# Block-diagonal products of a four-layer GNN, made in parts of the TensorE array instead of over zero blocks

## The chip, the cores and the metric

One NeuronCore of a Trainium2 chip. The metric is device time in us of one execution; lower is better. Times are medians of several executions; all executions quoted here were in the fast state. "PE" is the matmul engine (TensorE), "PEld" its loads of stationary matrices, DVE VectorE, ACT ScalarE, POOL GpSimd.

## The reference

128 graphs of 64 nodes with 256 features pass through four layers, each `x = x + layer(relu(layernorm(x)), adj)`. What the change touches in them is the product with something that is 64 x 64 for each graph:

```python
# layer 0 (4 heads of 64 features), layer 1 (1 head of 256): attention inside a graph
Hout = einsum('bijh,bjhf->bihf', softmax(...), Wh)
# layer 2: one relation ("loop") that selects edges with adj == 1
out = out + einsum('bnm,bmd->bnd', (adj_t == 1), vals)     # per graph
# layer 3: three rounds of a GRU over the graph
A = (adj != 0)
for i in range(3):
    m = h @ weight[i]
    aggr = einsum('bst,bsd->btd', A, m)                    # A^T per graph
    h = gru_cell(aggr, h, w_ih, w_hh, b_ih, b_hh)
```

(The kernel forms A^T h first and multiplies by `weight[i] @ w_ih.T` afterwards.)

## The kernel before

Everything is fp32. Two graphs share the 128 partitions ("a pair"), four pairs make a group, 16 groups go through the kernel. A planner written in the kernel records all operations, gives each an estimated cost and a due time, and emits them in a static order for every engine, so that attention layers of later groups fill the gaps of the GRU rounds ("the loop") of the group in front. Each fp32 matmul appears in the trace as two passes.

The products above were made for a pair at once, with a 128 x 128 matrix that has the two graphs on its diagonal and zeros elsewhere; such matrices are cleared once and only their diagonal blocks are written:

```python
def along(psum, hnat, abd, aT, c):             # A^T h, half c of the features
    pa = psum.tile([P, T], F32, name="tp")     # P = 128, T = 512
    for p in range(G):                         # G = 4 pairs
        nc.tensor.matmul(pa[:, p*P:(p+1)*P], hnat[:, p, c*P:(c+1)*P], abd[:, p, :], start=True, stop=True)
    nc.scalar.copy(aT[:, c, :], pa)

def aggregate(work, psum, lhsT, wv, heads):    # attention
    for p in range(n):
        po = psum.tile([P, 512], F32, name="mm")
        for h in range(heads):
            nc.tensor.matmul(pv[:, h, :], lhsT(p, h), wv[:, p, h, :], start=True, stop=True)
        # ... divide by the row of sums ...

# loop relation (layer 2)
    for i in range(2):
        nc.tensor.matmul(po[:, i, :], oh[:, p, :], v[:, p, :], start=True, stop=True)
```

In `along` the stationary operand is 128 nodes x 128 features of `hnat` and the moving one 128 nodes x 128 columns of `abd`. In attention the stationary operand is the 128 x 128 block matrix and 65 columns (four heads) or 257 (one head) move. The kernel uses eight banks of PSUM, the memory to which PE writes its results: five belong to named gates of the GRU, three are shared by all the rest.

## Time and profile before

| | kernel before |
|---|---|
| time, median | 1485.5 us (1484.1 to 1486.6) |
| span of the profiled run | 1483.7 us |
| busy: PE, DVE, ACT, POOL | 97%, 73%, 52%, 41% |
| steady period of a group (stores 1 to 12) | (1167.3 - 215.1) / 11 = 86.56 us |
| first store of a result | at 215.1 us |
| waits of PE between 215 and 1337 us | 0.6 us in all |

The row to read first is the last: in the middle PE runs without a stop, so any time that its stream gives or takes shows in the period. The prediction below shows the lines. One thing more is seen in the timeline of PE and PEld (columns: start, length, engine, what, count of passes):

```profile
722.67 0.60 PE L372 MATMUL rz<-aS,wc 128*128 128x256 f32 x2
722.89 1.08 PEld L372 LDWEIGHTS tp<-abd,hnat 128*128 128x128 f32 x8
```

The eight loads for an A^T h product begin at 722.89, while the pass before still runs; the first of its matmuls starts at 723.11. In a stream that uses the whole array, loads lie beneath running passes.

### The profile page before, as it was taken

To read this page: it belongs to the slowest core of one execution; us is meant where nothing else is said; L and a number is where in the kernel's file an instruction comes from. 1 tells how busy PE (TensorE), PEld (TensorE's weight loads), DVE (VectorE), ACT (ScalarE), POOL (GpSimd) and SP (SyncE) were. 2 spreads that over 40 slices of the span, in tenths; PEclk is the share of its full clock that TensorE was granted. 3 is DMA by queue.
4 is the path that set the end of the run, shared out by engine and by line. 5 is a ranking of instruction groups with operands and counts; after the bars stand their busy time and mean duration, and the time that the engine had idled before them with its cause. 6 is when DMAs were issued, how large, how long until landed. Compare 5 with 4: busy or idle time off the path is not lost.

```text
span 1483.7 us, 21159 instructions
## 1 busy us (share of the span) xinstructions
PE 1442.3 (97%) x6389; PEld 1065.7 (72%) x6389; DVE 1080.6 (73%) x2823; ACT 766.4 (52%) x1789; POOL 604.0 (41%) x752
## 2 busy tenths in 40 slices
PE   5979999999999999999999999999999999999997
PEld 4656777767777677777767777776777777676764
DVE  7667677786868778686877868687786868675644
ACT  3644645545454555545455554545555454554543
POOL 3522624433443454343345435334543433452522
PEclk7989999999999999999999999999999999999998
DMA  7010121122223122222312222231212222111000
GB/s 202 19 22 19 34 60 25 40 53 48 57 40 72 27 46 49 40 63 40 72 27 46 49 41 62 40 72 24 46 32 40 48 36 58 18 19 29 15 15 17
DMA packets 289635, 65.37 MB, mean 44 GB/s; under 512 B 265448, under 2 KB 287720, under 8 KB 289512
## 3 DMA queue, kind: packets, MB, share of 16 engines
q1 hardware_dynamic: 288952, 63.40, 20.2%
q8 instruction: 54, 0.88, 0.3%
q10 hardware_dynamic: 560, 0.52, 0.1%
q14 instruction: 69, 0.57, 0.1%
HBM read 25.96 MB, written 8.53 MB: 23 GB/s over the span
## 4 chain that ended last, share of the span: by engine, by line
PE 90%; DVE 6%; ACT 2%; SPq 1%; issue 1%; POOL 0%; DMA 0%; DVEq 0%; ACTq 0%
PE mm L372 22%; PE ry L372 22%; PE nh L372 11%; PE ni L372 10%; PE rz L372 10%; PE tp L372 9%; PE rm L372 5%; DVE hn L372 1%; DVE st L372 1%; SPq L372 1%; ACT hn L372 1%; DVE hT L372 1%; DVE d L372 0%; DVE o L372 0%; DVE z L372 0%
## 5 line engine op out<-in xcount | busy, mean ns | idle before, releaser
L372 POOL TENSOR_TENSOR d<-hT,t 128x256 f32<-128x256 f32 x192 | 151.7, 797 | 410.7 <-ACT t L372 410.7
L372 PE MATMUL ni<-aT,wc 128*128 128x512 f32 x384 | 195.7, 593 | 0.1
L372 PE MATMUL nh<-hT,whh 128*128 128x512 f32 x384 | 193.6, 593 | 0.0
L372 ACT COPY z<-ry 128x256 f32<-128x256 f32 x192 | 70.9, 369 | 188.0 <-PE ry L372 146.6
L372 DVE SCALAR_TENSOR_TENSOR t<-r,t 128x256 f32<-128x256 f32 x192 | 89.6, 467 | 90.4 <-ACT r L372 66.6
L372 ACT ACTIVATE z<-z,brz 128x256 f32<-128x256 f32 x192 | 96.8, 504 | 88.4 <-DVE z L372 86.4
L372 DVE TENSOR_TENSOR z<-rz,z 128x256 f32<-128x256 f32 x192 | 80.9, 421 | 78.6 <-PE rz L372 60.5
L372 POOL TENSOR_TENSOR xg<-xg,hn 128x1024 f32<-128x1024 f32 (+1 forms) x32 | 73.0, 2280 | 146.7 <-DVE hn L372 146.7
L372 DVE SCALAR_TENSOR_TENSOR d<-z,d 128x256 f32<-128x256 f32 x192 | 93.3, 506 | 33.2 <-ACT z L372 22.6
L372 PE MATMUL mm<-wl,hT 128*128 128x512 f32 x248 | 117.0, 593 | 0.2 <-ACT t L372 0.2
L372 PE MATMUL rz<-hS,whh 128*128 128x256 f32 x384 | 114.9, 381 | 1.9 <-DVE z L372 1.9
L372 ACT ACTIVATE hn<-xg,var,rstd 128x256 f32<-128x256 f32 x200 | 107.9, 594 | 16.8 <-DVE var L372 15.8
L372 PE MATMUL ry<-hS,wsum 128*128 128x256 f32 x384 | 115.6, 383 | 0.5 <-ACT z L372 0.5
L372 PE MATMUL ry<-aS,wsum 128*128 128x256 f32 x384 | 114.4, 380 | 0.0
L372 PE MATMUL rz<-aS,wc 128*128 128x256 f32 x384 | 114.3, 379 | 0.0
L372 PEld LDWEIGHTS tp<-abd,hnat 128*128 128x128 f32 x768 | 102.2, 192 | 15.4 <-issue 4.3
L372 POOL TENSOR_TENSOR hS<-hT 128x256 f32<-128x256 f32 x96 | 70.6, 741 | 96.2 <-PE ry L372 76.2
L372 PEld LDWEIGHTS ry<-hS,wsum 128*128 128x128 f32 x384 | 70.0, 190 | 54.8 <-issue 30.6
L372 ACT ACTIVATE t<-t,bi 128x256 f32<-128x256 f32 x192 | 93.6, 502 | 27.6 <-DVE t L372 26.7
L372 PE MATMUL tp<-abd,hnat 128*128 128x128 f32 x768 | 106.0, 275 | 0.0
L372 PEld LDWEIGHTS mm<-wh,eb 128*128 128x128 f32 x620 | 86.3, 195 | 18.9 <-issue 7.8
L372 DVE SCALAR_TENSOR_TENSOR hT<-d,t 128x256 f32<-128x256 f32 x192 | 95.8, 520 | 3.3
(192 smaller groups left out, 3193.6 us busy)
## 6 DMA issues: line engine op xcount, KB each, us to landing
hT<-hn SPq DMA_DIRECT2D x896, 32.0 KB
out_dram<-hnat SPq DMA_DIRECT2D x16, 512.0 KB
xg<-in_x_dram SPq DMA_DIRECT2D x15, 512.0 KB
hT<-row SPq DMA_DIRECT2D x28, 256.0 KB
at<-in_adj_dram SPq DMA_DIRECT2D x64, 32.0 KB
ag<-in_adj_dram SPq DMA_DIRECT2D x16, 128.0 KB
t<-row SPq DMA_DIRECT2D x28, 64.0 KB
ihn<-in_L_gnn_w_ih_dram SPq DMA_DIRECT2D x1, 768.0 KB
```

Of the source, the lines that this page charges most:

```text
L372: return do(*[real(a) for a in args], **{k: real(v) for k, v in kwargs.items()})
```

## The change

Its intent: compute only the diagonal blocks. TensorE can be used in parts. In the traces below a matmul whose operands lie on partitions 0 to 63 or 64 to 127 is listed with 64 rows of the array (`64*128`), one that also writes only 64 output partitions with 64 columns too (`64*64`), and several such products run side by side, with starts 0.007 us apart. So `A^T h` is made in two row parts (64 nodes each, 128 stationary columns), attention and the loop relation in four parts of 64 x 64. The change gives row parts that run at once different PSUM banks, so each set of products that are issued together (a "bundle") takes two of the three shared banks. The zero blocks, and the memsets that cleared them, go; the order of graphs within a group is changed so that the four parts meet. Core of the diff:

```diff
+    def beside(products, cost):        # emit all products of a bundle together, as one operation of the planner
     def along(psum, hnat, abd, aT, c):
-        pa = psum.tile([P, T], F32, name="tp")
+        pa, pb = psum.tile([P, G, N], F32, name="tp"), psum.tile([P, G, N], F32, name="tq")
+        products = []
         for p in range(G):
-            nc.tensor.matmul(
-                pa[:, p * P : (p + 1) * P], hnat[:, p, c * P : (c + 1) * P], abd[:, p, :],
-                start=True, stop=True,
-            )
-        nc.scalar.copy(aT[:, c, :], pa)
+            for half, ps in ((0, pa), (1, pb)):
+                b = slice(half * N, (half + 1) * N)
+                products.append((ps[:, p, :], hnat[b, p, c * P : (c + 1) * P], abd[b, p, :]))
+        beside(products, 700.0)
+        to = aT[:, c, :].rearrange("p (g a j) -> p a g j", a=2, j=N)
+        nc.scalar.copy(to[:, 0], pa)
+        nc.scalar.copy(to[:, 1], pb)
+    def aggregate_graphs(work, psum, t, wv, heads):
+        for u in range(n // 2):
+            banks = [psum.tile([P, 512], F32, name=name) for name in ("mm", "mn")]
+            for h in range(heads):
+                for a in range(2):
+                    for r in range(2):
+                        b, s, to = slice(r * N, (r + 1) * N), 2 * u + a, slice(a * N, (a + 1) * N)
+                        products.append((pv[r][to, h, :], t[b, s * heads + h, :], wv[b, s, h, :]))
+            beside(products, 800.0 if heads > 1 else 600.0)
# loop relation: likewise, one bundle of eight products in four parts
+            beside(products, 1050.0 * n / 4)
# planner: costs above; due times tuned anew
-        start, period = 88.0, 87.9
+        start, period = 94.8, 82.2
-    LATENCY = 165.1
+    LATENCY = 176.7
# (cut: layouts of hT and the edges, one more load of edges, min over 128 partitions at once)
```

More of the change, by code (lines that the diff above doesn't have):

```diff
@@ L152, in tile, with place @@
         return View(base, shape, (), [(0, n) for n in shape], list(range(len(shape))))
-    def place(self, base):
+    def place(self, base, taken):
         if self.real is None:
@@ L160, in place, with released @@
         live = [b for b in self.live.get(base.tag, ()) if b.left]
-        return base.tag if len(live) < base.bufs else None
-    def released(self, tag, base):
+        return base.tag if len(live) + taken.count(base.tag) < base.bufs else None
+    def released(self, tag, base, before):
         live = self.live.get(tag, ())
-        if len(live) < self.room(tag, base):
+        before -= self.room(tag, base) - len(live)
+        if before < 0:
             return 0.0
-        return min(b.end for b in live if not b.left) + Plan.LATENCY
+        return sorted(b.end for b in live if not b.left)[before] + Plan.LATENCY
     def room(self, tag, base):
@@ L220, in __getattr__, with all_of @@
         return getattr(self.nc, name)
+    @staticmethod
+    def all_of(view):
+        shape = view.base.make[0]
+        return View(view.base, shape, (), [(0, n) for n in shape], list(range(len(shape))))
     def kept(self, pool, shape, dtype, name):
@@ L317, in emit @@
                         if b.real is None:
-                            tag = b.pool.place(b)
+                            taken = [tag for x, tag in places.items() if x.pool is b.pool]
+                            tag = b.pool.place(b, taken)
                             if tag is None:
@@ L321, in emit @@
                             places[b] = tag
-                            t = max(t, b.pool.released(tag, b))
+                            t = max(t, b.pool.released(tag, b, taken.count(tag)))
                     else:
@@ L464 @@
     ar = adj.rearrange("b n m -> (b n) m").rearrange("(t q) m -> q t m", q=P)
-    tr = adj.rearrange("(u a g) i j -> a i u g j", a=2, g=2)
+    tr = adj.rearrange("(t r a) i j -> t a i r j", r=2, a=2)
+    er = adj.rearrange("(t r a) j i -> t r j a i", r=2, a=2)
     outr = out.rearrange("b n d -> (b n) d").rearrange("(t q) d -> q t d", q=P)
@@ L486, with by_graph, pair, layernorm_T @@
     brz = nc.kept(const, [P, 4], F32, name="brz")
-    def layernorm_T(work, psum, src, hT, natural=None):
+    def by_graph(hT):
+        return hT.rearrange("p k t -> p (k t)").rearrange("p (a k m j) -> p a k m j", a=2, k=K, j=N)
+    def pair(hT, k, s):
+        return by_graph(hT)[:, s % 2, k, s // 2 * 2 : s // 2 * 2 + 2].rearrange("p r j -> p (r j)")
+    def layernorm_T(work, psum, src, hT, natural=None, graphs=False):
         n = src.shape[1]
@@ L510, in layernorm_T, with layernorm_T_by_dma @@
                 nc.tensor.transpose(pt[:, p * P : (p + 1) * P], hn[:, p, k * P : (k + 1) * P], ident)
-            nc.scalar.activation(hT[:, k, :], pt[:, : n * P], AF.Relu)
+            to, out = hT[:, k, :], pt[:, : n * P]
+            if graphs:
+                to = by_graph(hT)[:, :, k]
+                out = out.rearrange("p (m a j) -> p a m j", a=2, j=N)
+            nc.scalar.activation(to, out, AF.Relu)
         if natural is not None:
             nc.vector.tensor_scalar(natural, hn, 0.0, None, op0=ALU.max)
-    def layernorm_T_by_dma(work, src, hT, natural=None):
+    def layernorm_T_by_dma(work, src, hT, natural=None, graphs=False):
         n = src.shape[1]
@@ L535, in layernorm_T_by_dma @@
             for j in range(P // S):
-                turned = hT[j * S : (j + 1) * S].rearrange("p k (n i c) -> p (k n) i c", n=n, c=S)
-                blocks = tb[i * S : (i + 1) * S].rearrange("p k n q -> p (k n) q")
-                nc.sync.dma_start(turned[:, :, i, :], blocks[:, :, j * S : (j + 1) * S])
+                turned, blocks = hT[j * S : (j + 1) * S], tb[i * S : (i + 1) * S]
+                if graphs:
+                    turned = by_graph(turned).rearrange("p a k m (b c) -> p a b (k m) c", b=2)[:, i // 2, i % 2]
+                else:
+                    turned = turned.rearrange("p k (n i c) -> p (k n) i c", n=n, c=S)[:, :, i]
+                blocks = blocks.rearrange("p k n q -> p (k n) q")
+                nc.sync.dma_start(turned, blocks[:, :, j * S : (j + 1) * S])
     def transpose_blocks(psum, dst, src, rblocks, scale=1.0):
@@ L567, in relational_weights, with emit @@
             nc.scalar.copy(w[:, f, D:], pm[:, :D])
+    def beside(products, cost):
+        def emit():
+            for product in products:
+                nc.nc.tensor.matmul(*[real(x) for x in product], start=True, stop=True)
+        if not nc.on:
+            return emit()
+        writes = list({id(x[0].base): x[0] for x in products}.values())
+        nc.note("PE", emit, cost, [Plan.all_of(x) for x in writes], [x for p in products for x in p[1:]])
     def elu_add(work, src, o, engine):
@@ L581, in block_diagonal, with values @@
             nc.vector.tensor_scalar(dst[b, :, b], src[b], scalar, None, op0=op)
-    def values(work, psum, src, heads, we, by_dma=False):
+    def values(work, psum, src, heads, we, by_dma=False, graphs=False):
         fo = D // heads
@@ L588, in values @@
         if by_dma:
-            layernorm_T_by_dma(work, src, hT)
+            layernorm_T_by_dma(work, src, hT, graphs=graphs)
         else:
-            layernorm_T(work, psum, src, hT)
+            layernorm_T(work, psum, src, hT, graphs=graphs)
         wh = work.tile([P, n, D + heads], F32, name="wh")
@@ L599, in values @@
                 nc.tensor.matmul(
-                    pm[:, : D + 2 * heads], hT[:, k, p * P : (p + 1) * P], we[:, k, :],
+                    pm[:, : D + 2 * heads], pair(hT, k, p) if graphs else hT[:, k, p * P : (p + 1) * P], we[:, k, :],
                     start=(k == 0), stop=(k == K - 1),
@@ L622, in aggregate @@
         return o.rearrange("p g h f -> p g (h f)")
+    def aggregate_graphs(work, psum, t, wv, heads):
+        fo = D // heads
+        n = wv.shape[1]
+        o = work.tile([P, n, heads, fo], F32, name="o")
+        for u in range(n // 2):
+            banks = [psum.tile([P, 512], F32, name=name) for name in ("mm", "mn")]
+            pv = [po[:, : D + heads].rearrange("p (h f) -> p h f", h=heads) for po in banks]
+            products = []
[5 more added lines that the diff above has]
+            beside(products, 800.0 if heads > 1 else 600.0)
+            for r in range(2):
+                rec = work.tile([P, heads], F32, name="rec")
+                nc.vector.reciprocal(rec, pv[r][:, :, fo])
+                nc.vector.tensor_tensor(
+                    o[:, 2 * u + r], pv[r][:, :, :fo], rec[:, :, None].to_broadcast([P, heads, fo]), ALU.mult
+                )
+        return o.rearrange("p g h f -> p g (h f)")
     def along(psum, hnat, abd, aT, c):
-        pa = psum.tile([P, T], F32, name="tp")
+        pa, pb = psum.tile([P, G, N], F32, name="tp"), psum.tile([P, G, N], F32, name="tq")
+        products = []
         for p in range(G):
-            nc.tensor.matmul(
-                pa[:, p * P : (p + 1) * P], hnat[:, p, c * P : (c + 1) * P], abd[:, p, :],
-                start=True, stop=True,
-            )
-        nc.scalar.copy(aT[:, c, :], pa)
+            for half, ps in ((0, pa), (1, pb)):
[5 more added lines that the diff above has]
+        nc.scalar.copy(to[:, 1], pb)
         return 0.9
@@ L667, in before_recurrence @@
             layernorm_T(work, psum, src, hT, natural=hnat)
-        block_diagonal(abd, adjacency, 0.0, ALU.not_equal)
+        nc.vector.tensor_scalar(abd, adjacency, 0.0, None, op0=ALU.not_equal)
         aT = work.tile([P, K, T], F32, name="aT")
@@ L877, in tile, with place @@
                 return view
-            def place(self, base):
+            def place(self, base, taken):
                 if base.tag in self.own:
-                    return super().place(base)
+                    return super().place(base, taken)
                 for tag in ("mt", *self.own) if self.early else ("mt",):
-                    if sum(1 for b in self.live.get(tag, ()) if b.left) < self.room(tag, base):
+                    live = sum(1 for b in self.live.get(tag, ()) if b.left)
+                    if live + taken.count(tag) < self.room(tag, base):
                         return tag
@@ L920 @@
         nc.scalar.dma_start(w0e[:, :, :D], rows(W0))
-        AT, XG, AG = [], [], []
+        AT, XG, AG, EG = [], [], [], []
         def load_group(g):
@@ L931, in load_group @@
                 for u in range(G // 2):
-                    nc.sync.dma_start(at[a * N : (a + 1) * N, u], tr[a][:, g * G // 2 + u])
+                    edges = tr[g * G // 2 + u, a]
+                    nc.sync.dma_start(at[a * N : (a + 1) * N, u], edges)
             AT.append(at)
@@ L939, in load_edges @@
             AG.append(ag)
+            eg = work.tile([P, G, N], I32, name="eg", bufs=2)
+            for r in range(2):
+                for u in range(G // 2):
+                    nc.sync.dma_start(eg[r * N : (r + 1) * N, 2 * u : 2 * u + 2], er[g * G // 2 + u, r])
+            EG.append(eg)
         bl = once.tile([P, 2 * D], F32, name="bl")
@@ L979, in attention_columns @@
                 )
-        unset = []
-        def blocks(name, n, pool=once):
-            t = pool.tile([P, n, P], F32, name=name)
-            unset.append(t)
-            return t
-        EB = [blocks("eb0", G * H), blocks("eb1", G)]
         wl = once.tile([P, K, 2 * D], F32, name="wl")
@@ L1009, in edge_bounds, with attention @@
             return mt
-        def attention(g, p0, n, layer, heads, we, pool, eb):
+        def attention(g, p0, n, layer, heads, we, pool):
             nh = n * heads
             src = XG[g][:, p0 : p0 + n]
-            wv, es = values(pool, psum, src, heads, we, g >= AHEAD)
+            wv, es = values(pool, psum, src, heads, we, g >= AHEAD, True)
             if layer == 0 and p0 == 0:
@@ L1023, in attention @@
             nc.scalar.activation(gd, es[:, :, heads:], AF.Exp, scale=ALPHA)
-            t = pool.tile([P, nh, N], F32, name="hT" if heads > 1 else "t")
+            t = pool.tile([P, nh, N], F32, name="t")
             if g < AHEAD:
@@ L1064, in attention @@
                 nc.vector.tensor_tensor(t[:, c], t[:, c], flat(fd, c), ALU.max)
-                for half in range(2):
-                    b = slice(half * N, (half + 1) * N)
-                    nc.vector.tensor_tensor(
-                        eb[b, c, b].rearrange("p (g h) i -> p g h i", g=m),
-                        t[b, c].rearrange("p (g h) i -> p g h i", g=m),
-                        mt[b, q : q + m, None, :].to_broadcast([N, m, heads, N]),
-                        ALU.min,
-                    )
-            o = aggregate(pool, psum, lambda p, h: eb[:, p * heads + h, :], wv, heads)
+                t4 = t[:, c].rearrange("p (g h) i -> p g h i", g=m)
+                edges = mt[:, q : q + m, None, :].to_broadcast([P, m, heads, N])
+                nc.vector.tensor_tensor(t4, t4, edges, ALU.min)
+            o = aggregate_graphs(pool, psum, t, wv, heads)
             elu_add(pool, src, o, nc.vector if g < 1 else nc.gpsimd)
-        def clear():
-            for t in unset:
-                nc.gpsimd.memset(t, 0.0)
         def first_weights():
@@ L1114, in loop_relation @@
             if g >= AHEAD:
-                layernorm_T_by_dma(pool, src, hT)
+                layernorm_T_by_dma(pool, src, hT, graphs=True)
             else:
-                layernorm_T(pool, psum, src, hT)
-            oh = OH[g % 2][:, p0 : p0 + n]
-            block_diagonal(oh, AG[g][:, p0 : p0 + n], 1.0, ALU.is_equal)
+                layernorm_T(pool, psum, src, hT, graphs=True)
+            oh = pool.tile([P, n, N], F32, name="oh")
+            nc.vector.tensor_scalar(oh, EG[g][:, p0 : p0 + n], 1.0, None, op0=ALU.is_equal)
             v = pool.tile([P, n, D], F32, name="v")
@@ L1123, in loop_relation @@
                 for k in range(K):
-                    nc.tensor.matmul(pm, hT[:, k, p * P : (p + 1) * P], wl[:, k, :], start=(k == 0), stop=(k == K - 1))
+                    nc.tensor.matmul(pm, pair(hT, k, p), wl[:, k, :], start=(k == 0), stop=(k == K - 1))
                 u = pool.tile([P, 2 * D], F32, name="u")
@@ L1128, in loop_relation @@
                 nc.vector.scalar_tensor_tensor(v[:, p, :], u[:, D:], 1.0, u[:, :D], op0=ALU.add, op1=ALU.mult)
-            for q in range(n // 2):
-                po = psum.tile([P, 2, D], F32, name="mm")
-                ps = slice(2 * q, 2 * q + 2)
-                for i in range(2):
-                    p = 2 * q + i
-                    nc.tensor.matmul(po[:, i, :], oh[:, p, :], v[:, p, :], start=True, stop=True)
-                nc.vector.scalar_tensor_tensor(src[:, ps, :], po, 0.0, src[:, ps, :], op0=ALU.max, op1=ALU.add)
-        MT, START = {}, {}
+            po = [psum.tile([P, n // 2, D], F32, name=name) for name in ("mm", "mn")]
+            products = []
+            for u in range(n // 2):
+                for a in range(2):
+                    for r in range(2):
+                        b, s = slice(r * N, (r + 1) * N), 2 * u + a
+                        products.append((po[r][a * N : (a + 1) * N, u, :], oh[b, s, :], v[b, s, :]))
+            beside(products, 1050.0 * n / 4)
+            for r in range(2):
+                to = src.rearrange("p (u r) d -> p r u d", r=2)[:, r]
+                nc.vector.scalar_tensor_tensor(to, po[r], 0.0, to, op0=ALU.max, op1=ALU.add)
+        MT, START, ABD = {}, {}, {}
         EARLY = [Layer(f"{i}e", early, {}) for i in range(3)]
-        EBE = [blocks("eb0e", 2 * H, early), blocks("eb1e", 2, early)]
-        OH = [blocks(f"oh{i}", G) for i in range(2)]
-        ABD = [blocks(f"abd{i}", G) for i in range(2)]
         def first_layer(g, p0, n, spare):
@@ L1146, in first_layer @@
                 pass
-            attention(g, p0, n, 0, H, w0e, *((EARLY[0], EBE[0]) if spare else (W[0], EB[0])))
+            attention(g, p0, n, 0, H, w0e, EARLY[0] if spare else W[0])
         def second_layer(g, p0, n, spare):
-            attention(g, p0, n, 1, 1, w1e, *((EARLY[1], EBE[1]) if spare else (W[1], EB[1])))
+            attention(g, p0, n, 1, 1, w1e, EARLY[1] if spare else W[1])
         def third_layer(g, p0, n, spare):
@@ L1164, in before @@
         def before(g):
-            START[g] = before_recurrence(W[3], psum, XG[g], AG[g], ABD[g % 2], g >= AHEAD)
+            ABD[g] = work.tile([P, G, N], F32, name="abd")
+            START[g] = before_recurrence(W[3], psum, XG[g], AG[g], ABD[g], g >= AHEAD)
         def recur(g):
             recurrence(
-                W[3], psum, START.pop(g), XG[g], ABD[g % 2],
+                W[3], psum, START.pop(g), XG[g], ABD[g],
                 lambda h: nc.sync.dma_start(outr[:, g * G : (g + 1) * G, :], h),
             )
-        nc.begin("clear")
-        clear()
         nc.begin("columns")
         first_weights()
-        nc.begin("weights", 18.0, 82.0)
+        nc.begin("weights", 18.0, 84.9)
         later_weights(early)
         layers = (first_layer, second_layer, third_layer)
-        start, period = 88.0, 87.9
+        start, period = 94.8, 82.2
         users = {}
@@ L1186 @@
             if g == 0:
-                units = [(0, 2, (3.7, 29.0, 52.5, 72.6)), (2, 2, (3.7, 31.0, 57.4, 75.8))]
+                units = [(0, 2, (-3.0, 30.1, 57.3, 72.2)), (2, 2, (4.1, 32.9, 59.6, 78.0))]
             elif g == 1:
-                units = [(0, 2, (26.1, 54.4, 86.1, 103.1)), (2, 2, (47.2, 70.3, 95.7, 123.8))]
+                units = [(0, 2, (28.7, 55.8, 87.9, 107.3)), (2, 2, (46.0, 70.1, 100.9, 126.4))]
             elif g == 2:
-                units = [(0, G, (76.1, 115.1, 174.5, 238.3))]
+                units = [(0, G, (74.9, 112.9, 175.1, 237.8))]
             else:
-                end = start + g * period - 25.0
-                units = [(0, G, [end - 63.0 * i for i in (3, 2, 1, 0)])]
+                end = start + g * period - 28.8
+                units = [(0, G, [end - 52.1 * i for i in (3, 2, 1, 0)])]
             for p0, n, at in units:
@@ L1205 @@
             at = start + g * period
-            nc.begin(("before", g), at - (13.0 if g == 0 else 18.9), at, [("recur", g - 2)] if g > 1 else [])
+            nc.begin(("before", g), at - (13.0 if g == 0 else 17.8), at, [("recur", g - 2)] if g > 1 else [])
             before(g)
@@ L1246, in general @@
                 psum = s3.enter_context(tc.tile_pool(name="gru_ps", bufs=1, space=PSUM))
-                abd = one.tile([P, G, P], F32, name="abd")
-                nc.gpsimd.memset(abd, 0.0)
+                abd = one.tile([P, G, N], F32, name="abd")
                 with tc.For_i(0, NP, G) as p0:
```

## The prediction

> **What bounds the kernel now.** I read the page first, then the table of stretches, the waits of the matmul engine, and its timeline in the middle of the run. The page names the engine:
>
> ```profile
> PE 1442.3 (97%) x6389; PEld 1065.7 (72%) x6389; DVE 1080.6 (73%) x2823; ACT 766.4 (52%) x1789; POOL 604.0 (41%) x752
> ```
>
> Busy time of pipelined matmuls is modelled, so I checked by stretches whether PE ever idles. I cut them where one group's result is stored and the next group's loop starts (the stores lie 86.5 us apart in the middle). Columns: length, then busy us of PE, PEld, DVE, ACT, POOL.
>
> ```profile
> 0.00:125.00 125.00, 100.33 (x410) 69.03 (x411) 86.08 (x258) 60.54 (x157) 47.30 (x73) 0.89 0.29 77
> ...
> 648.20:734.70 86.50, 86.50 (x390) 64.75 (x389) 65.66 (x174) 45.74 (x107) 36.58 (x44) 1.00 0.24 48
> 734.70:821.20 86.50, 86.50 (x390) 64.74 (x389) 65.64 (x174) 45.75 (x107) 36.58 (x44) 1.00 0.23 48
> ...
> 1412.00:1484.00 72.00, 59.66 (x253) 42.22 (x251) 30.61 (x68) 29.42 (x64) 20.48 (x28) 0.95 0.05 17
> ```
>
> In the middle PE never stops for a whole group and runs at full clock; the next engine, DVE, is busy 66 of 86.5 us. Between 215 and 1337 us the waits of PE come to two of 0.3 us. Only the first 125 us (25 us idle) and the last 72 us (12 us idle) are partly bound by latency. So in the middle, time taken from PE's stream comes off the span one for one, until DVE at about 66 us per group.
>
> What the changed products cost is read from starts in PE's timeline, not from busy times (columns: start, length, work; x counts passes, as each fp32 matmul appears as two instructions):
>
> ```profile
> 707.76 1.47 PE L372 MATMUL mm<-wh,eb 128*128 128x257 f32 x6
> 709.07 1.02 PE L372 MATMUL nh<-hT,whh 128*128 128x512 f32 x2
> 709.92 0.60 PE L372 MATMUL mm<-wh,eb 128*128 128x257 f32 x2
> 710.36 0.60 PE L372 MATMUL ry<-hT,wsum 128*128 128x256 f32 x2
> 710.79 0.59 PE L372 MATMUL rm<-aT,wc 128*128 128x256 f32 x2
> ...
> 723.11 1.05 PE L372 MATMUL tp<-abd,hnat 128*128 128x128 f32 x8
> 724.00 0.38 PE L372 MATMUL tp<-ident,m 128*128 128x128 f32 x2
> ...
> 736.38 2.91 PE L372 MATMUL mm<-wh,eb 128*128 128x65 f32 x24
> 739.12 0.65 PE L372 MATMUL ry<-hT,wsum 128*128 128x256 f32 x2
> 739.61 0.59 PE L372 MATMUL rm<-hT,whh 128*128 128x256 f32 x2
> 740.04 1.00 PE L372 MATMUL mm<-wh,eb 128*128 128x65 f32 x8
> 740.88 0.65 PE L372 MATMUL ry<-aT,wsum 128*128 128x256 f32 x2
> ```
>
> A pass over 512 columns costs 0.43 us (709.07 to 709.92 for two), over 256 columns 0.216, over 128 columns 0.111 (0.89 for eight): 0.84 ns a column. But 65 columns cost 0.114 (2.74 for 24), as much as 128. There the loading of a stationary matrix of 128 columns sets the pace, not the moving one.
>
> **What the Trainium skill says.** (1) "TensorE: Matmul & The Clock Gate", section "LDWEIGHTS (loading the stationary operand)": the load takes time by its columns, about 107 ns for 128, whatever the number of rows. The 0.114 us of the 65-column passes agrees. (2) The same page, "What overlaps and what doesn't" under "The mechanism": small products on different parts of the array run at once, with starts some 4 ns apart, but matmuls start and end in program order. No run yet shows this here. (3) The same page, section "Wait — 56ns, not 53.3ns?": starts are never closer than about 25 ns. The trace agrees: four tiny passes (`wq`, 10 columns, one stationary column) begin 26 ns apart. (4) "TensorEngine Tiling (Array Packing)", "Key Properties" and "Restrictions and Gotchas": changing the tiling drains the array, and row parts must write different PSUM banks. The kernel before has no tiling, so its trace cannot say what a drain costs; a lone pass of 128 columns lasts 0.275 us against a spacing of 0.111, so I estimate 0.16 us.
>
> **The change part by part.** Per group of four pairs of graphs, with a cost now and after. For "after" I use the costs that the diff itself gives its scheduler for the new bundles (0.70, 0.80, 0.60, 1.05 us). The scheduler's costs for old matmuls (118 ns a pass at least, 427 ns for 256 columns) are within some 5% of the trace, so I take these as fitted too, and check each against array time plus one drain.
>
> A^T h: six bundles a group (three layers, two halves). Now 8 passes, 0.89 us each, 5.34 in all. After: 16 passes over 64 columns, two row halves at once: 8 x 64 x 0.84 ns = 0.43, plus 0.16 is 0.59; the diff says 0.70. I take 0.70: 4.20 in all.
>
> Attention of four heads: now 32 passes, 2.74 + 0.84 = 3.58 us. After: two bundles of 32 passes, each at the 26 ns floor: 0.83; the diff says 0.80. 1.60 in all.
>
> Attention of one head: now 8 passes, 1.31 + 0.44 = 1.75. After: two bundles of 8 passes, four at once: 2 x 0.217 + 0.16 = 0.60, as the diff says. 1.20 in all.
>
> Loop relation: now 8 passes of 256 columns, 8 x 0.216 = 1.73. After: one bundle of 16 passes, four at once: 4 x 0.216 + 0.16 = 1.03; the diff says 1.05.
>
> Sum: 5.34 + 3.58 + 1.75 + 1.73 = 12.40 us now, 8.05 after: 4.35 us less a group, so a steady period of 82.15 instead of 86.5. Over 16 groups: 69.6 us.
>
> What lies beside it: ACT copies A^T h in two pieces of 256 columns instead of one of 512 (0.37 against 0.585 us a copy: 0.155 us more, six times a group; ACT is at 46 of 86.5). DVE does the `min` of attention and the edge masks once over 128 partitions instead of twice over 64: 4 x 0.686 + 2 x 0.42 + 4 x 0.285 us a group are halved, some 2.4 us less. Four small loads of edges a group are added, against DMA busy 24%. The clearing of zero blocks goes from POOL, about 5.8 us at the start; the first scale factor does not wait for it (POOL is idle 1.54 us before it), so nothing is gained there. None of this is on PE's path.
>
> What is taken off: group 0, and part of group 1, do their attention and loop products in the first 125 us, where PE idles anyway; of their 2 x 3.2 us I count half as lost, 3 us. Bundles need two of the three shared PSUM banks at once, where one was enough; for that I allow 0.2 us a group, 3 us. So 69.6 - 6 is about 64 us, and 1485.5 - 64 = 1421. The due times in the diff go from a period of 87.9 to 82.2, a little more than my 4.35; that pulls me down slightly, to **1418 us**.
>
> **The rivals.** First, **program order eats the overlap**. The two passes of one fp32 product use the same part of the array, and the second must wait for the first; if everything behind it waits too, only two parts ever run at once, and a bundle lasts about one pass per product. Then the one-head bundle is 4 x 0.217 + 0.217 + 0.16 = 1.24 us (now 0.87), the loop bundle 8 x 0.216 + 0.216 + 0.16 = 2.10 (now 1.73), the four-head bundle 16 x 0.058 + 0.22 = 1.15 (now 1.79), A^T h 0.70 (now 0.89). Net: 2 x 0.64 + 6 x 0.19 - 2 x 0.37 - 0.37 = 1.3 us a group, 21 us: about 1465. The diff's costs speak against it, the skill's program order for it.
>
> Second, **the weight loads become the bound of A^T h**. Its stationary parts keep 128 columns, so twice as many loads of the same length are needed. If loads of the two row halves did not overlap, a bundle would last 16 x 0.111 = 1.78 us, 0.89 more than now, or 85 us in all; with the other bundles still gaining 3.2 x 16 = 51 us the kernel would be slower, about 1520. Only the diff's 0.70 speaks against it.
>
> Third, **a new wait**: with two banks held until both ACT copies are done, PE finds no bank for the next group's work around A^T h, or drains cost twice (entering and leaving). There are 11 bundles a group; 0.16 us more for each is 28 us in all: about 1446. For it: eight banks, five tied to named gates. Against: PE's waits are nil now, so the schedule has other work to put in.
>
> **Range and chances.** The main line gives 1418; costs 0.1 us lower per bundle would give 1400, the third rival 1446. I give the rivals 10, 4 and 15%, and take 1398 to 1444 as the range. 2% is 1455.8: only the first two rivals miss it. So faster 0.90, same 0.08, slower 0.02.
>
> **What would show it.** Right: stores in the middle about 82 us apart; PE still without idle; A^T h bundles that take 0.6 to 0.8 us from their first start to the next group's start; four-head ones near 0.8; DVE busy 63 us a group. The first rival shows as loop bundles near 2 us; the second as A^T h bundles near 1.8; the third as PE waits on ACT `aT` or on DVE `o`, or a gap of over 0.3 us before the first full-array pass after a bundle. The prediction is wrong if the period stays above 84.5 us, or if the start before the first full loop (125 us now) grows by more than 10 us.

## The result, and the profile after

The changed kernel takes **1476.7 us** (1475.6 to 1477.4) against 1485.3 us of the kernel before (a fourth execution moved its median a little): a ratio of 0.9941 (95% interval 0.9924 to 0.9959), 0.6% less, where 4.5% was predicted. Ratios here are the mean time of one kernel's fast runs over that of the other's fast runs of the same rounds, so not quite the ratio of the medians quoted. The prediction's range (1398 to 1444) missed.

The page's first part, and the same kind of stretches as before (store to store in the middle; the start and the end):

```profile
PE 1428.2 (97%) x7925; PEld 981.2 (67%) x7925; DVE 1034.8 (70%) x2743; ACT 783.8 (53%) x1885; POOL 597.3 (41%) x744
...
0.00:125.00 125.00, 99.67 (x612) 63.26 (x613) 86.05 (x280) 63.85 (x168) 41.37 (x67) 0.93 0.31 81
634.00:721.10 87.10, 87.03 (x487) 59.58 (x486) 62.59 (x172) 48.60 (x117) 35.96 (x44) 1.00 0.25 50
721.10:808.80 87.70, 86.95 (x489) 60.18 (x488) 65.67 (x169) 47.57 (x114) 35.66 (x44) 1.00 0.24 49
1399.80:1473.80 74.00, 60.86 (x281) 41.53 (x279) 29.32 (x66) 29.64 (x68) 20.91 (x28) 0.94 0.05 16
```

The steady period has not moved: (1154.4 - 202.4) / 11 = 86.55 us. PE is nearly as full as before (busy for 948.0 of the 952.0 us between the first and the twelfth store, against 951.6 of 952.2), with about 487 passes in a group instead of 390. The whole difference of the span lies at the ends: the first store comes at 202.4 us instead of 215.1, and the stretch from the twelfth store to the last takes 312.9 us instead of 310.3.

What a bundle costs is read from its starts. An A^T h bundle, PE and PEld:

```profile
647.66 1.02 PE L380 MATMUL nh<-hT,whh 128*128 128x512 f32 x2
648.61 0.18 PEld L601 LDWEIGHTS tp<-abd,hnat 64*128 64x128 f32 x1 [0.76 <-ACT z L380]
648.61 0.32 PE L601 MATMUL tp<-abd,hnat 64*128 64x64 f32 x1
648.62 0.32 PE L601 MATMUL tq<-abd,hnat 64*128 64x64 f32 x1
648.77 0.27 PE L601 MATMUL tp<-abd,hnat 64*128 64x64 f32 x1
648.78 0.27 PE L601 MATMUL tq<-abd,hnat 64*128 64x64 f32 x1
648.88 0.27 PE L601 MATMUL tp<-abd,hnat 64*128 64x64 f32 x1
648.89 0.27 PE L601 MATMUL tq<-abd,hnat 64*128 64x64 f32 x1
...
649.45 0.27 PE L601 MATMUL tq<-abd,hnat 64*128 64x64 f32 x1
649.65 0.70 PE L380 MATMUL ry<-hT,wsum 128*128 128x256 f32 x2
650.19 0.59 PE L380 MATMUL ry<-aT,wsum 128*128 128x256 f32 x2
```

Three things are seen. The two row parts do run at once: their starts are 0.007 us apart. But the next pair comes only 0.11 us later, the same pace as one whole-array pass over 128 columns before, so eight pairs take what eight passes took. And the edges cost time: `nh` would have ended at 647.66 + 0.86 = 648.52, the bundle starts 0.09 later; its first load starts only with the bundle, not beneath `nh`; behind the bundle, the first two passes take 0.54 (649.65 to 650.19) instead of 0.43. Inside it, the first pair takes 0.16 instead of 0.11, and from the last pair to the pass behind it is 0.20. So 0.09 + 0.05 + 0.09 + 0.11 = 0.34 us of a bundle lie at its two changes of the division.

A loop bundle (four parts, 256 columns moving), and below it a four-head bundle (65 columns moving):

```profile
674.69 0.59 PE L380 MATMUL rz<-aS,wc 128*128 128x256 f32 x2
675.21 0.43 PE L601 MATMUL mm<-v,oh 64*64 64x256 f32 x1
675.22 0.43 PE L601 MATMUL mn<-v,oh 64*64 64x256 f32 x1
...
675.48 0.38 PE L601 MATMUL mm<-v,oh 64*64 64x256 f32 x1
...
675.70 0.38 PE L601 MATMUL mm<-v,oh 64*64 64x256 f32 x1
...
676.24 0.70 PE L380 MATMUL rz<-hS,whh 128*128 128x256 f32 x2
```

```profile
640.08 0.27 PE L601 MATMUL mm<-wh,t 64*64 64x65 f32 x1
640.09 0.27 PE L601 MATMUL mn<-wh,t 64*64 64x65 f32 x1
...
640.19 0.22 PE L601 MATMUL mm<-wh,t 64*64 64x65 f32 x1
...
640.25 0.22 PE L601 MATMUL mm<-wh,t 64*64 64x65 f32 x1
...
640.71 0.70 PE L380 MATMUL rz<-hS,whh 128*128 128x256 f32 x2
```

In the loop bundle rounds of four start 0.22 us apart: real fourfold overlap, 1.03 us for what took 1.73, and the same edges. In the four-head bundle they start 0.06 us apart behind the first, 0.63 us for 32 passes.

I summed these over ten groups (second to twelfth store): for each bundle the time from its first start to the start of the pass behind it, plus what the passes just before and just behind take beyond their usual spacing (0.09 us each). Per group, in us (the column "before" is the prediction's; summed from the trace in the same way it is 12.43):

| | before | predicted after | measured after | of it edges beside the bundle |
|---|---|---|---|---|
| A^T h, 6 bundles | 5.34 | 4.20 | 7.33 (1.22 each) | 1.10 |
| four heads, 2 | 3.58 | 1.60 | 1.81 (0.90 each) | 0.39 |
| one head, 2 | 1.75 | 1.20 | 1.59 (0.79 each) | 0.40 |
| loop relation, 1 | 1.73 | 1.05 | 1.21 | 0.19 |
| sum | 12.40 | 8.05 | 11.94 | 2.08 |

Attention and loop relation gain 2.45 us a group; A^T h loses 1.99. The rest, 0.46 us, is mostly used up by somewhat more waiting between passes (about 0.75 us a group against 0.46).

Why the gain sits at the start is shown only in part. Up to their first stores both kernels make the same products (attention of three groups, 1.5 loop relations, eight A^T h), and PE idles as long (26.8 and 26.7 us). With the bundles' costs above these products save about 4 of the 12.7 us. Some 5 us more may be the granted clock: it was 0.83 in the first 50 us and 0.93 from 100 to 150 us before the change, 0.86 and 1.00 after it, by the table of stretches (an estimate: 50 x 0.03 + 50 x 0.07). The rest, and why the clock differed, stays open; the due times of the first groups changed too.

### The profile page after: what moved, and what is told of

Same layout as the page of the kernel before. It is cut to its first block, busy times and chain, and to the rows that moved or that the text cites. A ratio compares the mean times of both kernels' runs of the same rounds, so it can differ in the third digit from the quotient of the medians.

```text
span 1473.8 us, 24378 instructions
## 1 busy us (share of the span) xinstructions
PE 1428.2 (97%) x7925; PEld 981.2 (67%) x7925; DVE 1034.8 (70%) x2743; ACT 783.8 (53%) x1885; POOL 597.3 (41%) x744
## 4 chain that ended last, share of the span: by engine, by line
PE 90%; DVE 5%; DMA 1%; SPq 1%; ACT 1%; issue 1%; POOL 0%; DVEq 0%
PE ry L380 22%; PE mm L380 15%; PE rz L380 11%; PE nh L380 11%; PE ni L380 11%; PE tp L601 6%; PE rm L380 6%; PE tp L380 4%; PE mm L601 3%; SPq L380 1%; DVE t L380 1%; DVE st L380 1%; DVE d L380 1%; DMA ihn<-in_L_gnn_w_ih_dram 1%; DMA hhn<-in_L_gnn_w_hh_dram 1%
## 5 line engine op out<-in xcount | busy, mean ns | idle before, releaser
L380 POOL TENSOR_TENSOR d<-hT,t 128x256 f32<-128x256 f32 x192 | 145.1, 763 | 492.9 <-ACT t L380 492.4
L380 DVE SCALAR_TENSOR_TENSOR t<-r,t 128x256 f32<-128x256 f32 x192 | 111.3, 583 | 62.6 <-ACT r L380 53.7
L380 POOL TENSOR_TENSOR hS<-hT 128x256 f32<-128x256 f32 x96 | 74.8, 783 | 136.0 <-PE ry L380 97.1
L380 DVE SCALAR_TENSOR_TENSOR d<-z,d 128x256 f32<-128x256 f32 x192 | 102.8, 545 | 36.7 <-POOL d L380 22.9
L601 PEld LDWEIGHTS tp<-abd,hnat 64*128 64x128 f32 x768 | 92.6, 187 | 48.8 <-issue 11.0
L601 PE MATMUL tp<-abd,hnat 64*128 64x64 f32 x768 | 105.8, 278 | 0.0
L601 PE MATMUL tq<-abd,hnat 64*128 64x64 f32 x768 | 105.8, 278 | 0.0
L380 POOL TENSOR_TENSOR aS<-aT,aS 128x256 f32<-128x256 f32 x96 | 75.9, 791 | 54.9 <-ACT aT L380 54.9
```

The source lines that it names most:

```text
L380: return do(*[real(a) for a in args], **{k: real(v) for k, v in kwargs.items()})
L601: nc.nc.tensor.matmul(*[real(x) for x in product], start=True, stop=True)
```

## The experiments

My theory after reading the two traces: (1) PE is the bound throughout. (2) Each pass of A^T h is paced by the load of its 128 stationary columns, which the row split doesn't shorten. (3) Each bundle has a fixed cost of about 0.35 us for entering and leaving the divided array: subtracting the rounds from the full costs leaves 1.22 - 8 x 0.109 = 0.35 for A^T h, 0.79 - 2 x 0.217 = 0.36 for one head, 1.21 - 4 x 0.216 = 0.35 for the loop relation. Rivals (told in full in the expectations): A, the period is set by something else; B, the other bundles gain nothing either and only the start got shorter; C, the streams of the row halves don't overlap; D, the fixed cost is a wait for inputs or banks.

### One part undone, one part alone

**A^T h back to whole-array products, the rest in parts.**

```diff
 # along, abd and block_diagonal as in the kernel before; two abd matrices cleared at the start
-        beside(products, 700.0)
+        nc.tensor.matmul(pa[:, p * P : (p + 1) * P], hnat[:, p, c * P : (c + 1) * P], abd[:, p, :], ...)
```

> The changed kernel with A^T h alone put back to whole-array products over zero blocks; attention and loop relation stay in parts. Main theory (PE-bound; in the changed trace an A^T h bundle holds PE 1.04 us plus about 0.18 us at its edges, 1.22 in all, against 0.89 for the whole-array form, so six of them lose 2.0 us a group while the other bundles gain about 2.45): 16 x 2.0 = 32 us less than the changed kernel, about 1445 us, steady period near 84.5 us. Rival A (the 86.6 us period is set by something other than PE, such as the schedule, DVE or loads, and no PE time shows): within 5 us of 1477. Rival B (the bundles of attention and loop gain nothing either, only the start got shorter): about 1477 too.

Measured: 1457.5 us, ratio to before 0.9825 (0.9809 to 0.9841). Undoing the A^T h part alone gains 19 us on the changed kernel, so rivals A and B fall. (This run also goes back to one bank and one ACT copy for each A^T h; the four-part run below keeps two of each and gains all the same.) It is 12 us short of the 1445 expected, and the steady period is 85.4 us instead of 84.5. The trace has more PE waits than that of the changed kernel (in the stretch from 285 to 1141 us the two longest of six lines, with total, times and longest):

```profile
PE tp L380 <- DVE hT L380: 7.5, 9, 0.9
PE rz L380 <- DVE z L380: 3.8, 10, 0.5
```

The changed kernel has 3.0 us on these two lines, from its first store to its twelfth. Besides, a four-head bundle takes 0.89 us on average here, against 0.71 there, because some stall on the way. The last run comes back to this.

**A^T h alone in row parts.**

```diff
 # the kernel before, with only these lines of the change
+        beside(products, 700.0)          # along in two row parts, abd without zero blocks
```

> The kernel before with A^T h alone made in row parts, as in the changed kernel; everything else as before, its due times too. Main theory: a loss of 6 x 0.33 us a group, 32 us: about 1517 us, steady period near 88.5. Rival A: within 5 us of 1485. If the A^T h bundles were as cheap as predicted (0.70 us) it would be about 1467.

Measured: 1549.2 us, ratio 1.0437 (1.0420 to 1.0455): a loss, as expected, but 65 us instead of 32. The period now alternates between 87 us and 95 to 96 us (stores at 490.4, 577.5, 672.3). The bundles cost the same 1.22 us as in the changed kernel; the rest lies mostly in every second group, with 3.2 us of idle PE and a granted clock of 0.98:

```profile
487.00:575.00 88.00, 88.00 (x436) 64.41 (x435) 65.82 (x169) 46.05 (x109) 38.09 (x44) 1.00 0.21 44
575.00:669.00 94.00, 90.79 (x440) 65.97 (x439) 69.56 (x177) 49.12 (x117) 35.86 (x44) 0.98 0.23 47
```

**The same, with the planner told the true cost.** The order is static and was planned with 0.70 us for a bundle that takes 1.22.

```diff
-        beside(products, 700.0)
+        beside(products, 1220.0)
```

> The kernel before with A^T h alone in row parts (1549 us, though the bundles alone explain only 1517), with its scheduler told that such a bundle takes 1.22 us instead of 0.70. If the rest of that loss came from an order planned with the wrong cost: 1515 to 1525 and no period of 96 us any more. If it comes from the two PSUM banks that a bundle holds, or other waits that the order can't hide: still above 1540.

Measured: 1524.7 us, ratio 1.0270 (1.0253 to 1.0287). 24.5 us of the extra loss were the order. What remains, 40 us over before, is near the 32 us of the bundles; the period still varies (88 to 92 us), so a few us of waits are left.

### What paces A^T h

**Four parts of 64 x 64 instead of two of 64 x 128.**

```diff
+            for f in range(2):
                 for half, ps in ((0, pa), (1, pb)):
                     b = slice(half * N, (half + 1) * N)
-                    products.append((ps[:, p, :], hnat[b, p, c * P : (c + 1) * P], abd[b, p, :]))
+                    to, d = slice(f * N, (f + 1) * N), c * P + f * N
+                    products.append((ps[to, p, :], hnat[b, p, d : d + N], abd[b, p, :]))
```

> The changed kernel with each A^T h product cut once more, into two stationary parts of 64 columns, so that four parts of 64 x 64 run side by side (32 passes a bundle instead of 16). Main theory (each pair of passes waits for the load of its 128 stationary columns, 109 ns; loads of different parts overlap): a round of four needs about 58 ns as in the four-head bundles, so the bundle shrinks from 1.04 to about 0.71 us plus edges 0.19, and the kernel takes about 6 x 0.33 x 16 = 32 us less, near 1445. Rival C (the moving streams of the two row halves do not overlap, 2 x 54 ns): the bundle stays at 1.04 us and the time at 1477. Rival A: 1477.

Measured: 1447.9 us, ratio 0.9757 (0.9741 to 0.9773). Twice as many passes, and the bundle is shorter, 0.625 us instead of 1.04:

```profile
638.31 0.27 PE L601 MATMUL tp<-abd,hnat 64*64 64x64 f32 x1
...
638.42 0.22 PE L601 MATMUL tp<-abd,hnat 64*64 64x64 f32 x1
...
638.48 0.22 PE L601 MATMUL tp<-abd,hnat 64*64 64x64 f32 x1
...
638.94 0.70 PE L380 MATMUL ry<-hT,wsum 128*128 128x256 f32 x2
```

Behind the first, a round of four (whose first starts are shown) takes 0.06 us. The stationary parts have half the columns; the moving data are as before. Rival C, which expected no change, falls.

**Half the moving columns** (wrong results on purpose).

```diff
-                products.append((ps[:, p, :], hnat[b, p, c * P : (c + 1) * P], abd[b, p, :]))
+                products.append((ps[:, p, : N // 2], hnat[b, p, c * P : (c + 1) * P], abd[b, p, : N // 2]))
```

> Wrong results on purpose: the changed kernel with only 32 instead of 64 moving columns in every A^T h product (the copies read those 32 twice). Main theory (paced by the load of 128 stationary columns): bundle stays near 1.04 us, time near 1477. Rival C (paced by moving data of two halves in turn): pairs at about 55 ns, bundle about 0.6 us, time near 1477 - 96 x 0.43 = 1436.

Measured: 1475.5 us (ratio 0.9940, 0.9924 to 0.9957), within 1.2 us of the changed kernel; the bundle takes 1.01 us. The pace is untouched:

```profile
649.93 0.29 PE L601 MATMUL tp<-abd,hnat 64*128 64x32 f32 x1
...
650.06 0.27 PE L601 MATMUL tp<-abd,hnat 64*128 64x32 f32 x1
...
650.17 0.27 PE L601 MATMUL tp<-abd,hnat 64*128 64x32 f32 x1
```

Pairs still come every 0.11 us, with half the moving data. Halving the stationary columns halves the time from one round to the next, halving the moving ones does nothing: the load of the stationary columns is what paces A^T h.

### The fixed cost of a bundle

Two kernels with the same needless product, once where the array is whole anyway, once amid the parts:

```diff
+        whole = (pb[:, G - 1, :], hnat[:, G - 1, c * P : (c + 1) * P], abd[:, G - 1, :])
+        products.insert(0, whole)        # the control; products.insert(4, whole) in the other
         beside(products, 700.0)
```

> Control for the next run. The changed kernel (row parts for A^T h) with one needless whole-array product of 64 columns put at the head of every A^T h bundle; a later product overwrites it, so results stay right. No further change between whole array and parts. Two passes at the pace of their 128-column loads: 0.22 us more a bundle, 96 bundles, 21 us: about 1498.

> The same needless whole-array product, but in the middle of every A^T h bundle, so that each bundle changes from parts to whole array and back once more. Main theory (a bundle has a fixed cost of about 0.35 us for entering and leaving the divided array, whatever it computes): 96 x 0.35 = 33 us over the control, about 1531. One drain of 0.16 us, as predicted: 15 us over it. Rival D (the fixed cost comes from waits for the bundle's inputs or banks and not from the division): no more than 3 us over the control.

Measured: 1491.3 us for the control (ratio 1.0044, 1.0028 to 1.0061; the extra passes cost 15 us rather than 21, since the first of their two loads lies beneath the long pass before, and the passes start 0.056 us apart) and 1523.4 us for the other (1.0257, 1.0240 to 1.0274). The difference, 32.1 us over 96 bundles, is **0.33 us for one more leaving and entering** of the divided array, with the same work and the same inputs and banks. It agrees with the 0.34 us that the edges of one bundle showed, and takes in loads that a change leaves uncovered: no run separates these from a drain of the array. Rival D expected 3 us, my prediction's single drain 15.

### The order

**Measured costs for the four-part version.**

```diff
-        beside(products, 700.0)
+        beside(products, 810.0)
-            beside(products, 800.0 if heads > 1 else 600.0)
+            beside(products, 900.0 if heads > 1 else 790.0)
-            beside(products, 1050.0 * n / 4)
+            beside(products, 350.0 + 870.0 * n / 4)
```

> The version with four 64 x 64 parts for A^T h (1447.9 us), with the scheduler's costs of the bundles set to what the traces measured, edges included (A^T h 0.81 us, four heads 0.90, one head 0.79, loop relation 0.35 + 0.87), instead of 0.70, 0.80, 0.60, 1.05. If the too low costs misled the static order (PE still waits about 1.3 us a group there): 5 to 15 us less, about 1438. If the order is as good as it can be with these due times: within 3 us of 1448.

Measured: 1479.6 us (ratio 0.9961, 0.9947 to 0.9975): a miss on both counts, 32 us *slower* than with the wrong costs. The kernel's products are the same; only the order differs, and in it bundles stall on the way (an A^T h bundle takes 0.78 us on average, against 0.625). Right costs with due times that were tuned for others gave a worse order.

**The same costs, with due times searched anew**, for both forms of A^T h. The search was over the planner's own estimate of its end; only these two results went to the chip.

```diff
-    LATENCY = 176.7
+    LATENCY = 171.8                      # four-part form
-        start, period = 94.8, 82.2
+        start, period = 94.9, 82.1       # whole-array form: 97.2, 82.2
-                units = [(0, G, [end - 52.1 * i for i in (3, 2, 1, 0)])]
+                units = [(0, G, [end - 52.9 * i for i in (3, 2, 1, 0)])]
# and shifts of up to 4 us in the first three groups and in the lead before a loop
```

> The four-part form of A^T h with the measured costs of the bundles (as in e5) and due times searched anew for these costs (start 94.9, period 82.1 and small shifts of the first groups, latency 171.8). If e5 was slow only because its due times belonged to other costs: PE waits fall below 1 us a group and the time goes below 1448, to about 1440. If the measured costs themselves lead to a worse order: about 1480 again.

> The whole-array form of A^T h with attention and loop relation in parts (e1, 1457.5 us, PE waits and stalled bundles there 1.5 to 2 us a group), with measured costs of the bundles and due times searched anew. If those waits came from the order: about 1447, near the 1445 that the bundles alone give. If not: within 3 us of 1457.

Measured: 1442.0 us (1440.2 to 1445.6), ratio 0.9715 (0.9702 to 0.9728), for the four-part form; 1444.2 us (1443.2 to 1445.5), ratio 0.9724 (0.9711 to 0.9737), for the whole-array form. Both beat the kernel before and the changed one. The second is where the bundles alone had put it (1445), and its waits of PE in the stretch from 293 to 1129 us are down to one line:

```profile
PE mm L601 <- DVE t L380: 0.5, 1, 0.5
```

So the 12 us by which the first experiment fell short were the price of an ill-fitting order: the products of the two kernels are the same. That the total meets 1445 so closely is partly luck. The steady period is 83.6 us (third to twelfth store), below the 86.6 - 2.45 = 84.1 that the bundles give, while the first store comes at 209.9 us, 7.5 later than in the changed kernel.

The four-part form has the cheaper bundle (0.625 + 0.18 = 0.81 against 0.89), which should be worth 6 x 0.08 x 16 = 8 us, but it is ahead by only 2 us, with ranges that overlap. Its steady period is even longer, 84.1 us against 83.6; its lead comes from the start (first store at 197.4 us). The 2.7 us of PE waits that are listed for its middle explain only part of that, so which form is better stays open.

## Why the prediction was wrong

- **PE as the bound: right.** With the same rest of the kernel, the time followed the bundles' cost: 1457.5 and 1447.9 us when A^T h was made cheaper, 1475.5 when work was removed that did not set the pace. DVE did fall, from 66.4 to 63.6 us a group (first to twelfth store), and the period did not move.
- **One-head attention and loop relation: right in mechanism; four heads: near by luck.** The prediction's 3.58, 1.75 and 1.73 became 1.81, 1.59 and 1.21, where it had 1.60, 1.20 and 1.05: 0.76 us a group too hopeful, 12 us in all. For four heads it let each of 32 passes wait for a floor of 26 ns and added no drain. Passes of different parts start 0.007 us apart, and 32 of them take 0.63 us; the edges that it left out, 0.19 us, bring that back to its 0.80.
- **The step that failed: "A^T h: ... 8 x 64 x 0.84 ns = 0.43, plus 0.16 is 0.59; the diff says 0.70. I take 0.70".** It counted moving columns only. The same prediction had read, from 65-column passes at 0.114 us, that the load of 128 stationary columns sets the pace of a short pass; A^T h kept its 128 stationary columns. Measured: 8 x 0.109 = 0.87 for the pairs and 1.22 in all. This term alone is 6 x 0.52 = 3.1 us a group, 50 of the 62 us that the sum 12.40 to 8.05 had too much; 0.44 of the 0.52 is the pace, the rest the fixed cost.
- **The second rival was nearer, but mis-sized.** It named the loads, but only for the case that those of the two halves don't overlap, with a bundle of 1.78 us. They overlap, and yet the pace is one load, 0.11 us a pair, so nothing is gained over the whole array.
- **The drain: "I estimate 0.16 us".** It is 0.33 to 0.36 us for entering and leaving together, as the third rival had it ("drains cost twice"), but that rival's 28 us were given 15%. Eleven bundles a group pay 3.9 us, where 1.8 was allowed.
- **Trusting the diff's costs.** "I take these as fitted too" was the choice that overruled the prediction's own evidence. Three of the four are near what a bundle took without its edges (0.71, 0.59 and 1.02 for 0.80, 0.60 and 1.05), but all are below what it took with them (0.90, 0.79, 1.21), and 0.70 is off by 0.52.
- **First rival (program order): wrong.** Rounds of four start 0.22 us apart in the loop bundle.
- **"About 3 us lost at the start": wrong way round.** The start is where the changed kernel won its time, 12.7 us at the first store (of which the bundles explain about 4).
- **Not foreseen: the order.** The same bundles took 1447.9, 1479.6 or 1442.0 us with three orders. The prediction treated a static order as free to refit.
- **Small slips.** The six A^T h bundles of a group come from three rounds of the GRU, not three layers, and the loop relation took 1.78 us before, not 1.73; neither matters.

What stays open: how much of the difference between bundles and span in the changed kernel is its own order (its row-part form was not run with new due times), and about 8 of the 12.7 us at its start.

## What to carry to other kernels

Before splitting a matmul over parts of the array, ask what paces its pass. Here, in fp32, passes with 32, 64 or 65 moving columns behind 128 stationary ones took 0.11 us, as long as those with 128: the load was the pace, and A^T h gained only from the split that halved its stationary columns. Count a fixed cost for every change between the whole array and parts (a third of a microsecond here), and split only where the bundle saves clearly more: four-head attention saved 0.89 us a bundle, one-head attention 0.08. In a statically ordered kernel, refit the order, costs and due times together, before judging a change: an order can move the time more than the change does, and new costs with old due times made it 32 us slower here.

## What the Trainium skill lacked or had wrong

- "TensorEngine Tiling (Array Packing)", "Key Properties", says that changing the tiling mode drains the engine, but gives no cost. Here it is 0.33 us for one entering and leaving (32.1 us over 96 bundles); this takes in that the first load of a bundle is not hidden beneath the pass before.
- The same page, "Theoretical Speedup", promises up to 2x where a dimension is 64 or less. It lacks the case where the load sets the pace: row parts with 128 stationary columns and 64 moving ones took 0.109 us a pair, against 0.111 us for one whole-array pass with the zeros; with 64 stationary columns a round of four took 0.06 us. "TensorE: Matmul & The Clock Gate", "LDWEIGHTS (loading the stationary operand)", has the rule (time by columns, not rows) and the traces agree with it.
- "TensorE: Matmul & The Clock Gate", "The mechanism", says in its list of what overlaps that loads do so with running matmuls only where the row group differs (its text before the list also names a background weight buffer). The traces differ from the "only": in the whole-array stream before, loads of 128 rows begin 0.22 us ahead of their own matmul, beneath a pass that uses the same rows. At a change of the division the load was not hidden.
